# A graph layer on one Trainium2 core: five picked stretches and 25 gathered chunks per 125 chunks, in place of four and 45

## Chip, core and metric

The kernel runs on one core of a Trainium2 chip. The metric is the device time of one execution in microseconds (us), the median over repeated runs. Before the change it is 2684.04 us over 14 runs, which lie between 2659.6 and 2693.91 us.

A core has engines that run side by side, each through its own list of instructions in order: TensorE (PE; its weight loads are shown apart as PEld), VectorE (DVE), ScalarE (ACT), GpSimd (POOL) and SyncE (SP), which only issues DMAs here. An engine waits where an instruction needs what another has not finished yet. TensorE writes to PSUM, and DVE or ACT have to take its results from there.

## What is computed

A message layer over a graph of 12,500 nodes with 128 features and 400,000 edges, sorted by target node:

```python
Xs = X[src]
m_data = Xs @ W_data.T + b_data
m_ctrl = Xs @ W_control.T + b_control
msg = jnp.where((edge_types == 0)[:, None], m_data, m_ctrl)
agg = jax.ops.segment_sum(msg, dst, num_segments=X.shape[0])
out = jax.nn.relu(agg + (X @ W_self.T + b_self))
result = _layernorm(X + out)
```

Everything is float32. `src` and the edge types are random; `dst` is sorted, so a stretch of edges belongs to a narrow band of target nodes.

## The kernel before, in words

The sums are formed first and multiplied by the weights afterwards: for every target node and both edge types the kernel adds up the rows `x[src]` and counts the edges, and the 128x128 weight products are done once for each node.

**Chunks, groups, stretches.** A chunk is 128 edges (`P`), and there are 3125 of them (`NC`). A group is 125 chunks (`GC`), and there are 25 groups (`NG`). Inside a group the generator `windows(g)` (line 160) lets two kinds of stretches alternate: a *gathered* stretch of `PC[i]` chunks and a *picked* stretch of `EC` = 20 chunks. With `PC = (12, 11, 11, 11)` a group has four of each, 45 gathered chunks and 80 picked ones. `NE = len(PC)` is the number of pairs in a group, and there are `NG * NE` = 100 pairs in all.

**The rows.** `x` is split once into three bfloat16 parts (high, middle, low), which together keep its float32 value. They stay in SBUF as `x3` (99 blocks of 128 nodes) and are also written to DRAM as `rows3`, 768 bytes for each node.

**A gathered chunk** (`gathered`, line 648) fetches its 128 source rows from DRAM. POOL issues one indirect DMA for each chunk (line 660) into a tile `msg` that holds `SB` = 4 chunks; six such tiles rotate (`bufs=6`, line 855). DVE builds a 0/1 matrix `psel` of 128 edges by 2 x 24 nearby target nodes (line 653 through line 443). TensorE then adds the three parts with three matmuls of 48 columns (line 616) and the counts with a fourth (line 674), each with its own 128x128 weight load. All chunks of a stretch add into one PSUM tile `sums`, and DVE adds that to `acc` at the stretch's end (line 646).

**A picked stretch** (`picked`, line 680, and `give_slots`, line 451) brings its 2560 edges' rows together without a DMA of rows. The edges are sorted by the block of 128 nodes in which their source lies: each of 98 blocks gets 32 slots, and up to 64 edges that find their block full go to an overflow list. The ranks of the edges inside their blocks come from 20 matmuls (`before`, line 483) and a series of DVE steps (lines 491 to 537). A second series of 20 matmuls (`put`, line 550) writes node and code of each edge into its slot. The node numbers go to DRAM and come back as `pick`, repeated over all 128 partitions (`spread`, lines 560 and 562, 800 KB), and DVE turns them into a 0/1 matrix (line 601). TensorE picks the rows out of `x3` with 98 matmuls of 384 columns that use 32 columns of the array each (`got`, line 694), for 25 tiles of 128 slots. ACT copies two such tiles at a time from PSUM to SBUF (`emsg`, line 705). TensorE adds them up with 75 matmuls of 176 columns (line 616) and counts with 25 (line 721). The overflow rows are fetched by one indirect DMA of 64 rows (`last`, line 713).

**The order.** Everything is recorded by hand: for each picked stretch `w` the function `merged` (line 137) sorts small units of work by a given place between 0 and 1 and runs them in that order. Merged are the seven units ("turns") of `picked(w)`, the slots of stretches `w+2` and `w+3`, the 0/1 matrix of `w+1`, the loads and preparations for the next groups, the closing of the previous group, and the gathered chunks, which are spread evenly over the whole program with a lag of two stretches (`LAG`, line 870). Each engine runs its part of the list in this order. A gathered chunk's DMAs are recorded where its `msg` tile begins, and POOL runs ahead of the matmuls as far as free `msg` tiles, free `last` tiles (two) and finished overflow lists (`idx`, line 589) let it.

**Loads and closing.** `load(g, kind)` (line 176) fetches sources, targets and types of a group's stretches, one DMA for each gathered stretch and array, and is issued two groups ahead from SP. Line 174 checks that all stretches of a kind stand 31 chunks apart, and `load` uses that 31 as its stride. `finish` (line 762) multiplies a group's sums by the weights, 125 nodes at a time, normalizes and writes out; for the last group, `soon` (line 759) says which blocks of nodes are closed after the last pair but one and which after the last. If an overflow list or a band of nodes would not fit, flags (lines 909 to 923) send the program to a slow general path, `long_path`.

Of the kernel before, what the change touches and what calls it, by code (L numbers as in the profile page):

```python
# [17 lines left out]
P = 128  # L18
# [4 lines left out]
GC = 125  # L23
NG = NC // GC
GN = P * GC * N // E
PC = (12, 11, 11, 11)
PB = 12
EC = 20
CQ = 4
NE = len(PC)  # L30
NWIN = 2 * NE
LAG = 2
DPC = P * N // E
PAD = 10
PW = DPC + 2 * PAD
EW = 88
AW = PW + DPC * (PB - 1)
WMAX = max(AW, EW)
# [5 lines left out]
NCELL = 4 * NQ  # L44
OVF = 64
TOP = 7
SB = 4
ACC_ROWS = 99 * P
EPS = 1e-5

assert sum(PC) + NE * EC == GC and NC % GC == 0 and NBLK == NCELL - 2 and max(PC) == PB


@with_exitstack
def kernel(
# [50 lines left out]
    with ExitStack() as sx:  # L106
        short_path(sx, tc, const, ident, eps, wT, brow, bad, x, src, dst, etype,
                   (w_data, w_ctrl, w_self), (b_data, b_ctrl, b_self), out)
# [38 lines left out]
def short_path(ctx, tc, const, ident, eps, wT, brow, bad, x, src, dst, etype, ws, bs, out):  # L147
    nc = tc.nc
# [11 lines left out]
    def windows(g):  # L160

        c = g * GC
        for i, n in enumerate(PC):
            yield "p", i, c, n
            yield "e", i, c + n, EC
            c += n + EC

    def edges(a, c, n):
        return a[c * P:(c + n) * P].rearrange("(p c) -> p c", c=n)

    rows_p = NE * PB
    raw = {}
    starts = {k: [c for kind, _, c, _ in windows(0) if kind == k] for k in "pe"}
    assert all(b - a == 31 for k in "pe" for a, b in zip(starts[k][k == "p":], starts[k][1 + (k == "p"):]))

    def load(g, kind):
        names = ("src", "dst", "typ")
        if kind == "e":
            raw[kind, g] = [ld.tile([P, NE, EC], I32, name=f"e{name}") for name in names]
            c = g * GC + starts["e"][0]  # L180
            for t, a in zip(raw[kind, g], (src, dst, etype)):
                at = a[c * P:(c + 31 * (NE - 1)) * P].rearrange("(i k) -> i k", k=31 * P)[:, :EC * P]
                nc.sync.dma_start(out=t[:, :NE - 1, :], in_=at.rearrange("i (p c) -> p i c", c=EC))
                nc.sync.dma_start(out=t[:, NE - 1, :], in_=edges(a, c + 31 * (NE - 1), EC))
        else:
            raw[kind, g] = [ld.tile([rows_p, P], I32, name=f"p{name}") for name in names]
            c = g * GC
            for t, a in zip(raw[kind, g], (src, dst, etype)):
                nc.sync.dma_start(out=t[:PB, :], in_=a[c * P:(c + PB) * P].rearrange("(c p) -> c p", p=P))
                for i in range(1, NE):  # L190
                    b = c + starts["p"][i]
                    nc.sync.dma_start(
                        out=t[i * PB:(i + 1) * PB, :], in_=a[b * P:(b + PB) * P].rearrange("(c p) -> c p", p=P)
                    )
# [11 lines left out]

    load_first("e")
    load(0, "e")
    load_first("p")


    near_i = keep.tile([rows_p, NG], I32, name="near_i")
    for kind, i, c, _ in windows(0):
        if kind == "p":
            nc.sync.dma_start(
                out=near_i[i * PB:(i + 1) * PB, :],
                in_=dst.rearrange("(o g e) -> o g e", o=1, g=NG)[:, :, c * P].to_broadcast([PB, NG]),
            )
    load(0, "p")


# [392 lines left out]
    def add_rows(out, msg, sel, start, stop):  # L614
        for j in range(3):
            nc.tensor.matmul(  # L616
                out, msg[:, j * D:(j + 1) * D], sel, start=(start and j == 0), stop=stop, skip_group_check=True
            )
# [29 lines left out]
    def gathered(g, i):  # L648
        n = PC[i]
        s = {}  # L650

        def choose():
            sel = sp.tile([P, n, 2 * PW], BF, name="psel")
            s["sel"] = select(sel, near_col, codes["p", g][1][:, i * PB:i * PB + n])

        def chunk(c):
            if c % SB == 0:
                s["msg"] = mp.tile([P, SB, 3 * D], BF, name="msg")
                for k in range(min(SB, n - c)):
                    nc.gpsimd.indirect_dma_start(  # L660
                        out=s["msg"][:, k, :], out_offset=None, in_=rows3[:, :],
                        in_offset=bass.IndirectOffsetOnAxis(
                            ap=codes["p", g][0][:, i * PB + c + k:i * PB + c + k + 1], axis=0
                        ),
                    )
            if c == 0:
                s["ps"] = sums()
                choose()
            sel = s["sel"][:, c].rearrange("p (t w) -> p t w", t=2)
            rows, cnt = (  # L670
                cells_of(s["ps"], AW, k).rearrange("p (t w) -> p t w", t=2)[:, :, DPC * c:DPC * c + PW] for k in range(2)
            )
            add_rows(rows, s["msg"][:, c % SB, :], sel, c == 0, c == n - 1)
            nc.tensor.matmul(cnt, one_col, sel, start=False, stop=(c == n - 1), skip_group_check=True)  # L674
            if c == n - 1:
                accumulate(g, 2 * i, s["ps"], AW, PW + DPC * (n - 1))

        return evenly([lambda c=c: chunk(c) for c in range(n)])
# [77 lines left out]

    soon = {NE - 2: (0, 1), NE - 1: (2, 3, 4)}
    assert (starts["p"][NE - 1]) * DPC - PAD >= 2 * (P - 3)  # L760

    def finish(g, ks):
        full = P - 3
# [85 lines left out]
    prep_e(0)  # L849
    merged(evenly(all_slots(0) + all_slots(1)), evenly(split_units))  # L850
    load(1, "e")
    load(1, "p")
    early.close()
    pro.close()
    mp = ctx.enter_context(tc.tile_pool(name="msg", bufs=6))
    sp = ctx.enter_context(tc.tile_pool(name="sel", bufs=2))
    fp = ctx.enter_context(tc.tile_pool(name="fin", bufs=2))
    merged(pick_matrix(0))
# [8 lines left out]
    for p in range(pairs):  # L867
        g, i = divmod(p, NE)
        for c, (_, u) in enumerate(gathered(g, i)):
            at = LAG + (p + (c + 0.5) / PC[i]) * (pairs - LAG) / pairs  # L870
            chunks.setdefault(int(at), []).append((at % 1, u))
        closed.setdefault(int(at), []).append(p)

    for w in range(pairs):
        g, i = divmod(w, NE)
# [188 lines left out]
```

## Time and profile before

| quantity | value |
|---|---|
| median of 14 runs | 2684.04 us (2659.6 to 2693.91) |
| the profiled execution | 2674.92 us |
| its span, first to last instruction | 2673.2 us |
| mean granted TensorE clock in it | 0.88 of full speed |
| instructions | 73115 |
| DVE busy | 1504.4 us, 4288 instructions |
| ACT busy | 1207.1 us, 2296 instructions |
| POOL busy | 1306.0 us, 1242 instructions |
| DMA moved | 236.87 MB, 89 GB/s on average |

The profile is of one execution. A group of instructions is shown by its line in the kernel, its engine, what it writes and reads, its shape and its count, then busy time, the mean length of one, and the idle time of the engine just before them with whoever ended it. "Issue" as the one who ended a wait means that the engine waited for nothing that the profile shows. The end of a matmul is modelled, so the distance from one matmul's start to the next tells more of TensorE's pace than the busy time does. The granted clock is what TensorE was given of its full clock. Of the chain of work that ended last, 62% is PE, 10% "issue", 10% a queue that the profile does not tell, 10% ACT and 5% DVE.

### The profile page before, as it was taken

The numbers are of one execution on the slowest core, as the hardware profiler recorded it, in microseconds if no ns is written. First come the engines' busy times: TensorE is split into PE (matmuls) and PEld (weight loads), VectorE is DVE, ScalarE is ACT, GpSimd is POOL, SyncE is SP. The second block draws the span as 40 slices with busy tenths as digits, with TensorE's granted clock in tenths as the row PEclk, the third lists the DMA queues.
The fourth block names the chain that finished last, engine by engine and source line by source line (L and its number), as shares of the span: only waits on it lengthen the run. The fifth ranks groups of instructions, "written<-read, shape, count | busy, mean of one in ns | idle before, by whom it ended". The sixth has DMA issues, their size and how long they took to land.

```text
span 2673.2 us, 73115 instructions
## 1 busy us (share of the span) xinstructions
PE 2090.1 (78%) x30669; PEld 1549.0 (58%) x30669; DVE 1504.4 (56%) x4288; ACT 1207.1 (45%) x2296; POOL 1306.0 (49%) x1242
## 2 busy tenths in 40 slices
PE   1678788788788887788888788787787887887877
PEld 0456566565566555665666566565565665665655
DVE  6665565555566555555555555564655555455542
ACT  3444445444454443444444444443544444444434
POOL 0544555545455554455455455445555545355451
PEclk9888999888888888888888888888999889888988
DMA  7433233222223332232232222232332222222221
GB/s 196 148 81 95 77 96 98 75 88 74 88 84 91 93 86 82 78 92 79 90 90 85 92 81 85 83 90 80 88 93 79 90 84 85 82 75 93 74 84 43
DMA packets 184175, 236.87 MB, mean 89 GB/s; under 512 B 79440, under 2 KB 151436, under 8 KB 183836
## 3 DMA queue, kind: packets, MB, share of 16 engines
q0 software_dynamic: 57200, 115.59, 15.6%
q1 hardware_dynamic: 113554, 109.92, 12.9%
q10 hardware_dynamic: 13082, 6.60, 0.9%
q8 instruction: 242, 3.96, 0.6%
q14 instruction: 97, 0.79, 0.1%
HBM read 215.35 MB, written 16.64 MB: 87 GB/s over the span
## 4 chain that ended last, share of the span: by engine, by line
PE 62%; issue 10%; another core or an unknown queue 10%; ACT 10%; DVE 5%; DMA 1%; POOL 0%; SPq 0%; DVEq 0%; ACTq 0%; POOLq 0%
PE sums L616 26%; PE got L694 20%; ACT emsg L705 7%; PE fin L800 4%; PE rk L483 3%; PE rk L550 2%; PE sums L721 2%; PE rk L575 1%; PE sums L674 1%; DMA xt<-in_x_dram 1%; DVE esel L443 1%; ACT h L829 1%; PE rk L570 1%; DVE prod L495 1%
## 5 line engine op out<-in xcount | busy, mean ns | idle before, releaser
L660 POOL DMA_INDIRECT msg<-rows,pidx x1125 | 1208.4, 1074 | 1214.2 <-PE sums L616 655.2
L705 ACT CAST emsg<-got 128x768 bf16<-128x768 f32 x1200 | 913.8, 802 | 916.4 <-PE got L694 365.4
L616 PE MATMUL sums<-esel,emsg 128*128 128x176 bf16 x7200 | 788.7, 261 | 99.7 <-issue 96.5
L694 PE MATMUL got<-x,pick 128*32 128x384 bf16 x9800 | 679.0, 364 | 160.1 <-ACT emsg L705 84.9
L616 PEld LDWEIGHTS <-emsg 128*128 128x128 bf16 x7200 | 610.4, 107 | 247.5 <-issue 242.5
L443 DVE TENSOR_TENSOR esel<-code_col,code 128x1408 bf16<-128x1408 bf16 (+1 forms) x400 | 291.9, 730 | 326.1 <-PE sums L616 166.7
L694 PEld LDWEIGHTS <-pick 128*32 128x32 bf16 x9800 | 248.6, 99 | 344.4 <-issue 249.4
L616 PE MATMUL sums<-psel,msg 128*128 128x48 bf16 x3375 | 251.3, 191 | 52.5 <-issue 42.1
L616 PEld LDWEIGHTS <-msg 128*128 128x128 bf16 x3375 | 206.1, 102 | 92.5 <-issue 86.4
L443 DVE TENSOR_TENSOR O<-cell_col,blk 128x2000 bf16<-128x2000 bf16 x100 | 118.1, 1181 | 210.5 <-issue 210.2
L721 PE MATMUL sums<-esel,one_col 128*32 128x176 bf16 x2500 | 182.0, 259 | 38.6 <-issue 37.1
L674 PE MATMUL sums<-psel,one_col 128*128 128x48 bf16 x1125 | 190.1, 189 | 12.0 <-issue 11.9
L483 PE MATMUL rk<-O,ltri 128*128 128x100 bf16 x2000 | 144.8, 230 | 60.1 <-issue 31.1
L491 DVE TENSOR_REDUCE ahead<-rk 128x100 bf16<-128x400 f32 x100 | 57.4, 574 | 230.5 <-remote 76.2
L483 PEld LDWEIGHTS <-ltri 128*128 128x128 bf16 x2000 | 120.2, 109 | 94.4 <-issue 59.1
L550 PE MATMUL rk<-rv,O 128*128 128x64 bf16 x2000 | 104.0, 205 | 58.9 <-issue 57.1
L713 POOL DMA_INDIRECT last<-rows,idx x100 | 93.6, 936 | 108.4 <-DMA xs<-in_x_dram 78.2
L721 PEld LDWEIGHTS <-one_col 128*32 128x32 bf16 x2500 | 89.2, 105 | 96.9 <-issue 67.6
L550 PEld LDWEIGHTS <-O 128*128 128x128 bf16 x2000 | 80.8, 105 | 107.5 <-issue 97.8
L585 ACT CAST code<-rk 128x50 bf16<-128x50 f32 x200 | 35.3, 176 | 228.4 <-PE rk L575 115.0
L545 DVE TENSOR_SCALAR om<-slot_col,rk 128x448 bf16<-128x448 bf16 x100 | 35.5, 355 | 178.3 <-PE rk L541 82.6
L601 DVE TENSOR_SCALAR pick<-pick,lane_f 128x1600 bf16<-128x1600 bf16 x200 | 127.0, 636 | 7.9 <-DMA pick<-there 5.3
(156 smaller groups left out, 2129.8 us busy)
## 6 DMA issues: line engine op xcount, KB each, us to landing
pick<-there SPq DMA_DIRECT2D x100, 800.0 KB
msg<-rows,pidx POOLq DMA_INDIRECT x1125
rows<-x SPq DMA_DIRECT2D x6, 1344.0 KB
xs<-in_x_dram SPq DMA_DIRECT2D x99, 62.5 KB
out_dram<-h SPq DMA_DIRECT2D x99, 62.5 KB
xt<-in_x_dram ACTq DMA_DIRECT2D x6, 896.0 KB
psrc<-in_src_dram SPq DMA_DIRECT2D x100, 6.0 KB
pdst<-in_dst_dram SPq DMA_DIRECT2D x100, 6.0 KB
```

The lines of the kernel that those rows point to most:

```text
L443: nc.vector.tensor_tensor(sel.rearrange("p n (w t) -> p n w t", t=2), col[:rows].rearrange("p (o w t) -> p o w t", o=1, t=2).to_broadcast( ...
L483: nc.tensor.matmul(cols[:, :, cells], ltri[:, a, :], s["O"][:, j:j + CQ, cells], start=(a == 0 and j == 0), stop=(j == EC - CQ), skip_grou ...
L550: nc.tensor.matmul(s["rk"][:, :2 * CAP], s["held"][:, c * NCELL:c * NCELL + P], s["rv"][:, c].rearrange("p v r -> p (v r)"), start=(c == 0 ...
L601: nc.vector.tensor_scalar(t, t, lane_f, None, op0=OP.is_equal)
L616: nc.tensor.matmul(out, msg[:, j * D:(j + 1) * D], sel, start=(start and j == 0), stop=stop, skip_group_check=True)
L660: nc.gpsimd.indirect_dma_start(out=s["msg"][:, k, :], out_offset=None, in_=rows3[:, :], in_offset=bass.IndirectOffsetOnAxis(ap=codes["p", ...
L674: nc.tensor.matmul(cnt, one_col, sel, start=False, stop=(c == n - 1), skip_group_check=True)
L694: nc.tensor.matmul(ps[CAP * a:CAP * (a + 1), :], slots[w]["pick"][:, a * NQ + q, :], x3[:, 4 * q + a - a0].rearrange("p j d -> p (j d)"), ...
L705: nc.scalar.copy(msg, ps[:, :, :3 * D])
L713: nc.gpsimd.indirect_dma_start(out=msg[:OVF, :], out_offset=None, in_=rows3[:, :], in_offset=bass.IndirectOffsetOnAxis(ap=slots[w]["idx"], ...
L721: nc.tensor.matmul(cells_of(s["ps"], EW, 1)[CAP * (q % 4):CAP * (q % 4 + 1), :], one_col[:, :CAP], s["sel"][q], start=(q < 4), stop=(q + 4 ...
L800: nc.tensor.matmul(s["ph"][:rows, i * D:(i + 1) * D], left, right, start=(j == 0), stop=(j == len(terms) - 1))
```

## The change

A group of 125 chunks is divided into five pairs in place of four: `PC` becomes `(5, 5, 5, 5, 5)`, with 20 picked chunks behind each. So there are 125 picked stretches in place of 100, and 625 gathered chunks in place of 1125. A `msg` tile holds five chunks, a whole gathered stretch, and four of them rotate in place of six of four chunks. The stride of stretches of one kind is 25 chunks in place of 31, and is now computed. For the last group three blocks of nodes are closed after the last pair but one and two after the last, in place of two and three. All widths that follow from these numbers (tables by `NE`, `PB`, `NWIN`, the width `AW` of a gathered stretch's sums) change with them. From line 172 on the changed kernel's lines have numbers higher by one.

```diff
-PC = (12, 11, 11, 11)
-PB = 12
+PC = (5, 5, 5, 5, 5)
+PB = 5
...
-SB = 4
+SB = 5
...
-    assert all(b - a == 31 for k in "pe" for a, b in zip(starts[k][k == "p":], starts[k][1 + (k == "p"):]))
+    gap = GC // NE
+    assert all(b - a == gap for k in "pe" for a, b in zip(starts[k][k == "p":], starts[k][1 + (k == "p"):]))
...
-                at = a[c * P:(c + 31 * (NE - 1)) * P].rearrange("(i k) -> i k", k=31 * P)[:, :EC * P]
+                at = a[c * P:(c + gap * (NE - 1)) * P].rearrange("(i k) -> i k", k=gap * P)[:, :EC * P]
                 nc.sync.dma_start(out=t[:, :NE - 1, :], in_=at.rearrange("i (p c) -> p i c", c=EC))
-                nc.sync.dma_start(out=t[:, NE - 1, :], in_=edges(a, c + 31 * (NE - 1), EC))
+                nc.sync.dma_start(out=t[:, NE - 1, :], in_=edges(a, c + gap * (NE - 1), EC))
...
-    soon = {NE - 2: (0, 1), NE - 1: (2, 3, 4)}
-    assert (starts["p"][NE - 1]) * DPC - PAD >= 2 * (P - 3)
+    soon = {NE - 2: (0, 1, 2), NE - 1: (3, 4)}
+    assert (starts["p"][NE - 1]) * DPC - PAD >= 3 * (P - 3)
...
-    mp = ctx.enter_context(tc.tile_pool(name="msg", bufs=6))
+    mp = ctx.enter_context(tc.tile_pool(name="msg", bufs=4))
```

## The prediction

> **What bounds the kernel now.** First the page: which engine is busiest, and with what.
>
> ```profile
> span 2673.2 us, 73115 instructions
> PE 2090.1 (78%) x30669; PEld 1549.0 (58%) x30669; DVE 1504.4 (56%) x4288; ACT 1207.1 (45%) x2296; POOL 1306.0 (49%) x1242
> ...
> L660 POOL DMA_INDIRECT msg<-rows,pidx x1125 | 1208.4, 1074 | 1214.2 <-PE sums L616 655.2
> L705 ACT CAST emsg<-got 128x768 bf16<-128x768 f32 x1200 | 913.8, 802 | 916.4 <-PE got L694 365.4
> ```
>
> POOL and ACT mostly wait for PE, so PE sets the pace. Next the view of who PE waits for:
>
> ```profile
> PE sums L616 <- issue: 141.0, 292, 1.2
> PE got L694 <- ACT emsg L705: 84.9, 191, 1.5
> PE got L694 <- issue: 59.8, 130, 1.2
> PE rk L550 <- issue: 57.1, 100, 1.4
> ```
>
> All PE waits that name another engine come to 161 us after the first pick; those for nothing shown ("issue") to 347 us. Whether the second kind belongs to picked or to gathered work decides this case. Stretches of time (length, then busy PE, PEld, DVE, ACT, POOL with counts, granted clock, DMA share, GB/s):
>
> ```profile
> 84.00:104.00 20.00, 18.43 (x317) 13.35 (x315) 19.93 (x59) 14.03 (x25) 17.26 (x10) 1.00 0.34 105
> 106.00:124.00 18.00, 7.45 (x45) 3.56 (x44) 2.02 (x6) 1.60 (x2) 13.74 (x15) 0.64 0.28 76
> 2630.00:2656.00 26.00, 24.20 (x417) 18.72 (x414) 6.64 (x17) 17.40 (x27) 0.00 (x0) 1.00 0.02 5
> 1097.40:1100.80 3.40, 2.99 (x30) 1.98 (x30) 3.37 (x7) 2.86 (x5) 2.63 (x3) 0.50 0.28 77
> ```
>
> From 106 us POOL issues 15 gathers back to back (1.25 us apart), and PE gets 45 matmuls done in 18 us. After 2630 us POOL is silent: 417 matmuls in 26 us, full clock, and no "issue" wait at all. At 84 to 104 us the gathers come 2 us apart, and PE runs freely. POOL's timeline shows the usual pattern, runs of gathers:
>
> ```profile
> 1009.42 0.95 POOL L660 DMA_INDIRECT msg<-rows,pidx  x1 [7.10 <-PE sums L616]
> 1010.67 0.95 POOL L660 DMA_INDIRECT msg<-rows,pidx  x1 [0.30 <-issue]
> 1011.93 0.95 POOL L660 DMA_INDIRECT msg<-rows,pidx  x1 [0.30 <-issue]
> 1013.18 0.95 POOL L660 DMA_INDIRECT msg<-rows,pidx  x1 [0.31 <-issue]
> ```
>
> I laid the "issue" idles over 0.1 us (768, together 355 us) on POOL's runs (gaps under 1 us). Runs, moved 2 us later, cover 1609 us of the span and hold 354.8 of the 355.1 us. So PE starves while gathers are in flight, a few us into a run; its clock then falls. The loss belongs to runs of gathers. What undisturbed work costs, from PE's timeline at full clock:
>
> ```profile
> 86.59 0.83 PE L694 MATMUL got<-x,pick 128*32 128x384 bf16 x16
> 87.25 0.25 PE L721 MATMUL sums<-esel,one_col 128*32 128x176 bf16 x4
> 87.44 1.08 PE L616 MATMUL sums<-esel,emsg 128*128 128x176 bf16 x12
> 88.45 0.83 PE L694 MATMUL got<-x,pick 128*32 128x384 bf16 x16
> ...
> 1047.26 0.23 PE L616 MATMUL sums<-psel,msg 128*128 128x48 bf16 x3
> 1047.34 0.18 PE L674 MATMUL sums<-psel,one_col 128*128 128x48 bf16 x1
> 1047.45 0.83 PE L694 MATMUL got<-x,pick 128*32 128x384 bf16 x16
> ```
>
> Start to start: 16 picks 0.66 us, 4 counts 0.19, 12 sums 1.01, a gathered chunk 0.19.
>
> **The ledger before.** A picked stretch, undisturbed: 98 picks 4.04, 25 counts 1.19, 75 sums 6.31, the 20 matmuls of line 483 1.04 (94.69 to 95.73 us), the 20 of line 550 0.58 (92.43 to 93.01), lines 570 and 575 0.45 (93.48 to 93.93): 13.6 us. A gathered chunk: 0.10 to 0.20 in such places; I take 0.15. Closing 100 blocks of nodes: 1.4 us each, from the three at the end (2658.1 to 2663.0 us, a small one among them); 140 us. So 100 x 13.6 + 1125 x 0.15 + 140 = 1669 us of work. PE has 2673.2 less 71 before the first pick and 7 after its last instruction: 2595. Lost: 926 us, 161 of it to other engines, and 765 to the runs: starving, and the low clock behind it.
>
> What a run costs: between 1 us after its first gather and 3 us after its last (or the next run), I added each matmul's distance to the next less what that pair takes undisturbed. 41 runs of three: 1.4 us on average; 127 of four 2.9; 56 of five 4.2; 18 of eight (two of four with a small gap) 5.2; 10 of nine 7.0. About 0.5 of each is waits for other engines, counted above: 0.9, 2.4, 3.7, 4.7, 6.5. With the first run of 26 (24 us) that makes some 750 us, which agrees.
>
> **The change, part by part.**
>
> *25 more picked stretches* add 25 x 13.6 = 340 us of PE work. Waits for other engines go with them: 161 x 1.25 = 201. DVE gets (1504 - 78 before 100 us) / 100 = 14.3 us a stretch, so some 1850 us; ACT (1207 - 47) / 100 = 11.6, so some 1500. Both stay below PE's 1.25 x 13.6 x 100 = 1700 plus the rest; ACT is the nearer one in a free stretch (17.40 of 26 us above). If it held PE up more often, half as much again on 161 would be 80 us, and no row shows less than the share of now; 0 and 40 are my ends for the extra, and I take 0. The 25 more `pick` broadcasts (800 KB) are hidden: they are issued a stretch before they are needed, and PE's waits for `pick` are two, both before 75 us.
>
> *500 fewer gathered chunks* take 500 x 0.15 = 75 us off (50 to 100 by the bounds). DVE's `psel` (430 ns, 100 of them) and stretch sums (416 ns for 256 columns) become 125 smaller ones, off PE's path.
>
> *Preparations by group*: `load` issues 15 small DMAs for gathered stretches where it issued 12, the tables at the start 2 and 1 more; all on SP, two groups ahead or beside the loading of `x` before 71 us. 0 us; each could cost at the start at most the length of one small landing, some 2 us (`there`'s landing is waited for 62.3 us in 57 waits, 1.1 each): 0 to 6 us.
>
> *The end*: two blocks in place of three behind the last stretch, 1 us less.
>
> *The runs.* POOL's list in the changed program repeats `last`, then five `msg`, for every stretch. `last` of stretch w waits for its overflow list, made at the end of stretch w-2, and for its buffer, read at the same point. Behind it five gathers are queued whose tile (four rotate) was read out a stretch or more earlier: nothing holds them. So each stretch gets one run of six at its start; before, the six smaller tiles came free one by one and gave runs of three to five, 2.6 a stretch. The gathers now released are ready two stretches early, so nobody waits for them. Gathers fall from 1225 to 750, but runs grow. A run of six is not in the trace. Lower end: the starving goes by the gather and the low clock by the run. The excess ended by "issue" in that tally is 509 us, 0.42 for each gather, and the rest of 765 is 256, 1.0 for each of 256 runs; 6 x 0.42 + 1.0 = 3.5, and since `last` brings 64 rows and not 128, 3.4. Upper end: the step from four to five (1.3) goes on: 5.0. From five to nine the step is 0.7, so 4.4, which I take: it is nearest to the rows beyond five. 125 x 4.4 = 550 us.
>
> Sum: 71 + 7 + 1700 + 625 x 0.15 + 140 + 201 + 550 - 1 = 2762 us, against 2673 by the same ledger. The median lies 2684.04 / 2674.92 = 1.0034 above the profiled execution, so 2771; I say 2770.
>
> Two pages of the Trainium skill bear on the runs. The page "Runtime: NRT & Kernel Launch" (Instruction fetch mechanics) says that instructions come in blocks of 16 KiB and that this is mostly hidden; the trace has 242 packets of that queue (3.96 MB) and yet 347 us in which PE waits for nothing shown, so the rule as it stands does not hold here. By it the runs' starving, if it is one of instructions, would be hidden, and the ledgers without runs (2212 and 1908 us) would make the change 304 us slower. The page "TensorE: Matmul & The Clock Gate" (The HAM clock gate) says that the clock is either full or half, and halves after an idle window of about 3.4 us; the slice from 1097.4 us has 0.50 for 3.4 us. By that rule a run of six, if it starves PE so long, halves the clock once in every stretch, an estimate of 125 x 1.7 = 213 us from the page's figures.
>
> **The rivals.**
>
> *Faster: the starving goes by the gathered row.* Then a run costs 3.4 us and the sum is 2762 - 125 x 1.0 = 2637, 2646 as a median. For it: runs of eight cost 0.6 a gather, no more than the average of now (765 / 1225 = 0.62), and fewer runs are fewer falls of the clock. Against: 0.9, 2.4, 3.7 for three, four, five is far from proportional. Place: the start of each picked stretch. It decides below (2673 - 2212) / 125 = 3.7 us a run, 2212 being the sum without runs.
>
> *Much slower: runs of six starve PE to the end.* At 5.0 us a run, and ACT holding PE up half as often again (40 us of the 80), 2762 + 75 + 40 = 2877, 2887 as a median. For it: 45 matmuls in 18 us in the long run. Against: that run has 15 full gathers on end.
>
> *Slower by the average stretch.* If the loss went with picked work, a gathered chunk at its mean distance (0.29, waits included) leaves (2595 - 140 - 326) / 100 = 21.3 us a stretch: 25 x 21.3 - 500 x 0.29 = 388 more, 3071 as a median. Against: the free stretch after 2630 us.
>
> *It does something else*: a flag sends it to the slow path. From the inputs the fullest overflow list has 63 of 64 places (57 before), the fullest lane 5 of 7, the widest band 84 of 88; so not.
>
> **How the numbers follow.** Forecast (3.7 to 4.8 us a run) 0.52, faster rival 0.28, much slower 0.14, average stretch 0.05, the rest 0.01. What this measurement can tell from no change is about 0.3%, 8 us. The faster rival reaches into that with 0.06 of its 0.28, the forecast with 0.02: faster 0.22, same 0.08, slower 0.70. The range runs from the lower end of the runs' cost, 2645, to 2865, which is short of the full upper case; about 0.08 is left out below and 0.12 above. The forecast's own range is 2685 to 2820 (3.7 to 4.8).
>
> **What would show it.** POOL: 625 `msg` and 125 `last`, in runs of six that begin where `last` is released. PE: "issue" idles in one place of each stretch, 350 to 450 us in all, and a stretch of some 21 us from first pick to first pick. ACT: 1500 casts, the wait of picks for them near 106 us. Wrong if the issue idle falls below 300 us (faster rival) or the picks wait over 150 us for ACT; wrong in its root if "issue" idles appear outside the runs.

## The result, with the profile after

The changed kernel takes 2823.52 us, the median of 10 runs (2811.1 to 2844.36); the kernel before took 2682.33 us over 47 runs beside it. The ratio is 1.0542, with an interval of 1.0513 to 1.0571: slower by 141 us. The profiled execution took 2827.83 us at a span of 2826.1 us. The forecast was 2770 us.

Chips differ in this case. On three of the chips of the experiments the kernel before takes 1915 us, on another 2690 us, much as in the result; every ratio below is to the kernel before on the same chip.

The page of the changed kernel: first the engines, then the groups that answer to those shown of before (busy time, mean ns of one, idle time before them and what ended most of it).

```profile
span 2826.1 us, 82925 instructions
...
PE 2293.2 (81%) x34919; PEld 1718.6 (61%) x34919; DVE 1793.6 (63%) x5167; ACT 1459.1 (52%) x2746; POOL 798.5 (28%) x767
...
L706 ACT CAST emsg<-got 128x768 bf16<-128x768 f32 x1500 | 1142.9, 802 | 911.1 <-PE got L695 412.6
L661 POOL DMA_INDIRECT msg<-rows,pidx x625 | 672.8, 1077 | 1810.5 <-PE sums L675 1243.3
...
L714 POOL DMA_INDIRECT last<-rows,idx x125 | 121.6, 973 | 173.9 <-DMA ptyp<-in_edge_type_dram 77.8
```

PE is busier, with a quarter more casts on ACT and 500 gathers fewer on POOL, as the diff says. The means of one cast (802 ns) and one gather (1077 ns, 1074 before) have hardly changed. What PE waits for (us in total, times, longest):

```profile
PE got L695 <- ACT emsg L706: 128.1, 135, 6.3
PE got L695 <- issue: 81.3, 105, 9.8
PE sums L617 <- issue: 77.7, 149, 1.2
PE rk L551 <- issue: 52.3, 93, 1.2
```

The waits that end with "issue" fell from 347 us to 270 us in all, but picks now wait 128 us for ACT, against 85 us. POOL's timeline (start, length, then in brackets the idle time before and who ended it) shows a whole run:

```profile
1011.42 1.01 POOL L661 DMA_INDIRECT msg<-rows,pidx  x1 [14.95 <-PE sums L675]
1012.74 0.98 POOL L661 DMA_INDIRECT msg<-rows,pidx  x1 [0.30 <-issue]
1014.02 0.94 POOL L661 DMA_INDIRECT msg<-rows,pidx  x1 [0.30 <-issue]
1015.27 0.95 POOL L661 DMA_INDIRECT msg<-rows,pidx  x1 [0.30 <-issue]
1016.53 0.98 POOL L661 DMA_INDIRECT msg<-rows,pidx  x1 [0.30 <-issue]
1017.81 0.97 POOL L714 DMA_INDIRECT last<-rows,idx  x1 [0.30 <-DVE top L513]
1036.20 1.70 POOL L661 DMA_INDIRECT msg<-rows,pidx  x1 [17.42 <-ACT emsg L706]
```

One run of six, then nothing for 17 us, then the next run. Stretches of time around that run (length, then busy PE, PEld, DVE, ACT, POOL with counts, granted clock, DMA share, GB/s):

```profile
1014.00:1017.00 3.00, 1.88 (x29) 1.10 (x27) 1.92 (x7) 0.00 (x0) 2.37 (x3) 1.00 0.26 73
1017.00:1020.00 3.00, 0.73 (x4) 0.47 (x5) 2.77 (x14) 0.00 (x0) 1.48 (x2) 1.00 0.29 77
1020.00:1023.40 3.40, 3.34 (x22) 3.32 (x22) 1.88 (x11) 2.13 (x5) 0.00 (x0) 0.62 0.29 30
...
1027.00:1030.00 3.00, 2.94 (x58) 2.25 (x56) 2.76 (x14) 2.08 (x5) 0.00 (x0) 1.00 0.00 0
```

This is the loss in four rows. From the third gather on PE gets 29 matmuls done in 3 us, then 4; ACT does nothing at all, while DVE works on. Then the work comes back, but the clock has fallen: 0.62 is the mean of a row in which PE had half speed from 1020.84 us on, for 3.4 us. Seven microseconds later all is well again (58 matmuls in 3 us). PE's own timeline in the second and third row:

```profile
1017.22 0.24 PE L722 MATMUL sums<-esel,one_col 128*32 128x176 bf16 x1 [1.06 <-issue]
...
1018.63 0.31 PE L617 MATMUL sums<-esel,emsg 128*128 128x176 bf16 x2 [1.00 <-issue]
1020.06 0.84 PE L617 MATMUL sums<-esel,emsg 128*128 128x176 bf16 x9 [1.11 <-issue]
```

Twelve matmuls that belong together, and take 1.01 us undisturbed, are broken up by pauses of a microsecond in which nothing that the profile shows is missing.

What ACT waits for at that place is called "remote", which means that its wait ended with a signal whose sender the view could not name:

```profile
1012.30 1.54 ACT L706 CAST emsg<-got 128x768 bf16<-128x768 f32 x2
1020.31 1.50 ACT L706 CAST emsg<-got 128x768 bf16<-128x768 f32 x2 [6.46 <-remote]
```

The trace's semaphore records tell the sender: the cast at 1020.31 us follows a signal of PE at 1020.24, and the last pick before it that raises this signal ended, as modelled, at 1016.10.

Where the time came from and went, by the same count as in the prediction (each matmul's distance to the next, less what such a pair takes undisturbed; the excess is put down to what ended the pause, and the excess without a pause to the low clock). The first row is the ledger's prices times the counts (125 x 13.6 + 625 x 0.15 + 140 for the changed kernel), so it is reckoned and not measured, and the small rows below it are rough:

| us of PE's steady time | before | after | difference |
|---|---|---|---|
| undisturbed work | 1669 | 1934 | +265 |
| excess ended by "issue" | 509 | 369 | -140 |
| low clock | 257 | 223 | -34 |
| excess ended by ACT's casts | 121 | 159 | +38 |
| the rest | 39 | 60 | +21 |
| sum | 2595 | 2745 | +150 |

The remaining 3 us of the spans' difference (152.9) lie before the first pick, after the last matmul and in rounding. So by this table the change pays 265 us of work and gets back only 115 us of the loss to gathers. Two of its rows can be checked another way. In the stretches at half speed, matmul distances without a pause exceed what such pairs take on a chip without the loss by 281 us before and 245 after, which is near the table's -34. PE's pauses over 0.1 us that name another engine than ACT's casts are 75 us before and 63 after, so the +21 of the last row is not confirmed.

### The profile page after: what moved, and what is told of

Its sections match the earlier page's. It is cut to its first block, busy times and chain, and to the rows that moved or that the text cites. A ratio compares the mean times of both kernels' runs of the same rounds, so it can differ in the third digit from the quotient of the medians.

```text
span 2826.1 us, 82925 instructions
## 1 busy us (share of the span) xinstructions
PE 2293.2 (81%) x34919; PEld 1718.6 (61%) x34919; DVE 1793.6 (63%) x5167; ACT 1459.1 (52%) x2746; POOL 798.5 (28%) x767
## 4 chain that ended last, share of the span: by engine, by line
PE 61%; DVE 11%; another core or an unknown queue 10%; ACT 8%; issue 7%; DMA 2%; SPq 0%; DVEq 0%; ACTq 0%
PE sums L617 26%; PE got L695 18%; ACT emsg L706 6%; PE fin L801 4%; PE rk L484 4%; PE rk L551 3%; PE sums L722 2%; DVE esel L444 1%; DVE pick L602 1%; PE rk L576 1%; DVE prod L496 1%; DMA pick<-there 1%; DMA xt<-in_x_dram 1%; DVE rm L444 1%
## 5 line engine op out<-in xcount | busy, mean ns | idle before, releaser
L706 ACT CAST emsg<-got 128x768 bf16<-128x768 f32 x1500 | 1142.9, 802 | 911.1 <-PE got L695 412.6
L661 POOL DMA_INDIRECT msg<-rows,pidx x625 | 672.8, 1077 | 1810.5 <-PE sums L675 1243.3
L617 PE MATMUL sums<-esel,emsg 128*128 128x176 bf16 x9000 | 936.2, 258 | 65.9 <-issue 63.7
L695 PE MATMUL got<-x,pick 128*32 128x384 bf16 x12250 | 785.9, 353 | 222.4 <-ACT emsg L706 128.1
L617 PEld LDWEIGHTS <-emsg 128*128 128x128 bf16 x9000 | 747.2, 105 | 252.5 <-issue 248.7
L444 DVE TENSOR_TENSOR esel<-code_col,code 128x1408 bf16<-128x1408 bf16 (+1 forms) x500 | 364.9, 730 | 408.2 <-PE sums L617 240.8
L695 PEld LDWEIGHTS <-pick 128*32 128x32 bf16 x12250 | 294.0, 98 | 432.9 <-issue 303.4
L617 PE MATMUL sums<-psel,msg 128*128 128x48 bf16 x1875 | 159.0, 189 | 16.9 <-issue 14.0
L496 DVE TENSOR_TENSOR prod<-O,ahead 128x2000 bf16<-128x2000 bf16 x125 | 149.5, 1196 | 2.6
L617 PEld LDWEIGHTS <-msg 128*128 128x128 bf16 x1875 | 126.3, 102 | 29.9 <-issue 26.8
```

Of the source, the lines that this page charges most:

```text
L444: nc.vector.tensor_tensor(sel.rearrange("p n (w t) -> p n w t", t=2), col[:rows].rearrange("p (o w t) -> p o w t", o=1, t=2).to_broadcast( ...
L496: nc.vector.tensor_tensor(prod, s["O"], ahead.rearrange("p (o j) -> p o j", o=1).to_broadcast([P, EC, NCELL]), op=OP.mult)
L617: nc.tensor.matmul(out, msg[:, j * D:(j + 1) * D], sel, start=(start and j == 0), stop=stop, skip_group_check=True)
L661: nc.gpsimd.indirect_dma_start(out=s["msg"][:, k, :], out_offset=None, in_=rows3[:, :], in_offset=bass.IndirectOffsetOnAxis(ap=codes["p", ...
L695: nc.tensor.matmul(ps[CAP * a:CAP * (a + 1), :], slots[w]["pick"][:, a * NQ + q, :], x3[:, 4 * q + a - a0].rearrange("p j d -> p (j d)"), ...
L706: nc.scalar.copy(msg, ps[:, :, :3 * D])
```

## The experiments

### What is left where the gathers disturb nobody

The first question was what the runs are worth. One pair of kernels leaves the gathers of `msg` out; another has tiles of one chunk, so that gathers are released singly. The edits, for the kernels without gathers and for those with small tiles (before: `SB = 4` to 1, `bufs=6` to 24):

```diff
-                s["msg"] = mp.tile([P, SB, 3 * D], BF, name="msg")
-                for k in range(min(SB, n - c)):
-                    nc.gpsimd.indirect_dma_start(
...
+                s["msg"] = still
...
-    mp = ctx.enter_context(tc.tile_pool(name="msg", bufs=4))
+    still = keep.tile([P, SB, 3 * D], BF, name="still")
+    nc.vector.memset(still, 0.0)
```

```diff
-SB = 5
+SB = 1
...
-    mp = ctx.enter_context(tc.tile_pool(name="msg", bufs=4))
+    mp = ctx.enter_context(tc.tile_pool(name="msg", bufs=20))
```

> The changed kernel without the 625 gathers of msg: its matmuls read one tile of zeros, so the gathered edges' rows are left out of the sums; the 125 gathers of last stay. If the loss belongs to runs of gathers (forecast), TensorE's waits for nothing shown fall from 273 us to under 30, and the time falls by the excess that lies in the runs, some 600 us, to 2210-2270 us. If the loss belongs to picked work (the rival by the average stretch), the time stays within 50 us of 2823.

> The kernel before without the 1125 gathers of msg, which leaves the gathered edges' rows out of the sums in the same way. Forecast: 2682 less some 740 us, 1920-1990 us, and the changed kernel without gathers stands some 300 us above it (340 for 25 picked stretches, 75 less for gathered chunks, 40 for waits). If the loss belongs to picked work: 2630-2680.

> The changed kernel with msg tiles of one chunk, 20 of them in place of four of five: the same gathers, rows and buffer space, but each gather is released by a matmul of its own. If the length of a run decides (forecast), the runs of six break up into ones and twos, which cost next to nothing, and the time falls to 2230-2400 us. If the loss goes by the gathered row (the faster rival's premise, 0.6 us a gather), it stays within 60 us of 2823.

> The kernel before with msg tiles of one chunk, 24 of them in place of six of four. If the length of a run decides, the runs of three to five break up; 1225 gathers at 1.25 us are 1530 us, so they stand closer than in the changed kernel and some starving may stay: 2000-2350 us. If the loss goes by the gathered row: within 60 us of 2682.

They came on a chip where the kernel before takes 1915.4 us, so that the ratios answer another question than the one asked:

| kernel | us | ratio to before | interval |
|---|---|---|---|
| after without gathers | 2158.02 | 1.1272 | 1.1213 to 1.1331 |
| before without gathers | 1848.73 | 0.9656 | 0.96 to 0.9713 |
| after, one-chunk tiles | 2200.22 | 1.1503 | 1.1453 to 1.1553 |
| before, one-chunk tiles | 1923.14 | 1.0041 | 1.0013 to 1.0069 |

On this chip PE has, in all four kernels together, one pause over 0.1 us that ends with "issue" (0.2 us), and the granted clock is 0.98 or more on the mean of each profiled execution, even where up to 287 gathers follow each other with no gap of a microsecond (in before with one-chunk tiles). Leaving the gathers out saves 67 us in the kernel before. So the next experiment ran the changed kernel itself, and its small tiles again, on such a chip.

> The changed kernel itself beside the kernel before on one chip. The four runs so far fell on a chip on which the kernel before takes 1915 us and no wait of TensorE for nothing shown lies in its gather runs. If this run falls on such a chip, the ledger without runs holds: before 1915, this one 1915 plus 340 for 25 picked stretches less 75 for 500 gathered chunks, some 2180, ratio 1.13 to 1.15. If it falls on a chip like the first, 2823 against 2682, ratio 1.05. If picked stretches were not the price (loss by gathers alone), the ratio on the free chip would be near 1.00.

> The changed kernel with 20 msg tiles of one chunk, again. On a chip that starves TensorE during gather runs: 2230-2400 us if the length of a run decides, within 60 us of 2823 if the loss goes by the gathered row. On a free chip: within 1% of the changed kernel, since no run costs anything there.

The changed kernel took 2191.21 us against 1914.97, a ratio of 1.1458 (1.1397 to 1.1518): 276 us slower, where the table of work above gives 265. With one-chunk tiles it took 2195.86 us (1.1492, 1.1426 to 1.1557), which is the same. Lines of the changed kernel's page, its waits of PE and POOL's timeline on this chip:

```profile
span 2182.0 us, 82925 instructions
...
PE 1970.1 (90%) x34919; PEld 1556.2 (71%) x34919; DVE 1776.0 (81%) x5167; ACT 1453.8 (67%) x2746; POOL 876.3 (40%) x767
...
PEclk9999999999999999999999999999999999999999
```

```profile
PE rk L542 <- DVE over_n L517: 128.7, 96, 21.8
...
PE got L695 <- ACT emsg L706: 7.9, 28, 0.4
```

```profile
1000.56 0.96 POOL L661 DMA_INDIRECT msg<-rows,pidx  x1 [7.46 <-PE sums L675]
1001.82 0.95 POOL L661 DMA_INDIRECT msg<-rows,pidx  x1 [0.30 <-issue]
1003.08 0.95 POOL L661 DMA_INDIRECT msg<-rows,pidx  x1 [0.30 <-issue]
1004.33 1.34 POOL L661 DMA_INDIRECT msg<-rows,pidx  x1 [0.30 <-issue]
```

The same runs of six (115 of them, 119 in the result), 1.25 us from gather to gather in the lines shown, and none of PE's unexplained pauses. Two things follow. First, a run of gathers does not by itself stop PE: it is a property of some chips that PE starves in it. Second, with the same 1500 casts the picks wait 7.9 us for ACT and not 128.1. The 128 us are no lack of ACT's speed; they come with the runs. The trace of the result shows how: in its idle times, ACT's casts wait 371 us (115 times) for a "remote" signal, which never occurs in this run. Laid on POOL's runs moved 2 us later, which cover 985 us of the span, ACT's idles after 75 us that end with "remote" or "issue" fall inside them for 405 of 418 us.

The missing signal is PE's. After 75 us the trace of the result keeps 3020 signals of PE, and 360 of them come more than 1 us after the modelled end of the last matmul that raises them, 358 of these in or up to 4 us behind a run. In this run it is 2 of 3018. ACT's and DVE's signals are that late twice each in both traces, at the end of the program. So ACT does not stop by itself in the runs: it waits for PE, whose work is reported late, and PE in turn waits for ACT. Since the ends of matmuls are modelled, the trace does not say whether the matmul ended late or only its signal.

What holds PE up most in the undisturbed kernel can be read there too: DVE is at 81%, and PE's largest wait is for the ranks' sums (`over_n`).

The next experiment asked whether the tile sizes have a part of their own: the changed kernel with the old tiles (`SB = 4`, `bufs=6`), and the kernel before with five-chunk tiles (`SB = 5`, `bufs=5`).

> The changed kernel with the old msg tiles, six of four chunks: of the change only the split into five pairs of 20 picked and 5 gathered chunks is left. A stretch's gathers then come as four and one. On a free chip (before near 1915): within 1% of the changed kernel, 2170-2215 us, since tiles cost nothing there. On a chip that starves TensorE in gather runs (before near 2680): runs of four or five in place of six, 100-250 us under the changed kernel's 2823 if the length of a run decides, within 60 us of it if the loss goes by the gathered row.

> The kernel before with msg tiles of five chunks, five of them: of the change only the tiles. On a free chip: within 1% of the kernel before. On a starving chip: runs of five (a stretch of 12 as 5, 5, 2, one of 11 as 5, 5, 1) in place of four, 50-150 us over 2682 if the length of a run decides, within 30 us if the loss goes by the gathered row.

On a chip where before takes 1915.33 us they took 2184.74 us (1.1452, 1.1331 to 1.1573) and 1919.22 us (1.0033, 1.0007 to 1.006). Undisturbed, the split into five pairs makes the whole difference, and the tiles make next to none. The runs did not come as expected: with the old tiles 117 of 126 are runs of six, so here they follow from the split and not from the tiles' size. Where gathers disturb, neither of the two kernels was run, so the tiles' own part there is not known from them.

### The two kinds of work apart, where the gathers disturb

Then a chip on which before takes 2689.73 us. Both kernels without their whole gathered side, so that only picked stretches, preparations and closing are left:

```diff
-        def choose():
...
         def chunk(c):
-            if c % SB == 0:
...
+            pass
...
-    mp = ctx.enter_context(tc.tile_pool(name="msg", bufs=4))
```

> The kernel before without its whole gathered side: no gathers, no 0/1 matrices, no matmuls and no sums of gathered chunks, whose edges are left out of the result. Measures the gathered chunk on TensorE. Without the gathers alone it took 1849 us; if a gathered chunk costs 0.15 us of TensorE (the ledger), 1125 of them come off: 1680 us. If they lie in gaps that other waits leave anyway, 1760-1849.

> The changed kernel without its whole gathered side, in the same way. Without the gathers alone it took 2158 us. Ledger: 625 x 0.15 off, 2064 us; the difference to the kernel before without its gathered side is 25 picked stretches, 340 us by their undisturbed work alone, some 385 with their waits for DVE and ACT.

They took 1713.59 us (0.6364, 0.6322 to 0.6405) and 2082.55 us (0.7734, 0.7684 to 0.7784), 34 and 19 us over what the ledger gave. Page and waits of PE of the first:

```profile
span 1711.2 us, 62013 instructions
...
PE 1544.4 (90%) x26169; PEld 1187.5 (69%) x26169; DVE 1404.6 (82%) x4088; ACT 1198.5 (70%) x2296; POOL 97.3 (6%) x117
```

```profile
PE rk L541 <- DVE over_n L516: 86.4, 65, 21.8
...
PE got L671 <- ACT emsg L682: 8.4, 28, 0.6
```

No pause of PE over 0.1 us ends with "issue", the mean clock is 0.994, and the picks wait 8.4 us for ACT, on the chip on which they starve when gathers run. The 25 stretches more cost 2082.55 - 1713.59 = 369 us, 14.8 us each, 1.2 over the 13.6 of work in the ledger. The gathered side is the rest of each whole kernel: 2689.7 - 1713.6 = 976 us before, 2823.5 - 2082.6 = 741 us after. Its own work is small: the kernels without gathers, which keep the gathered matmuls, lie 135 us (1848.7 - 1713.6, for 1125 chunks) and 75 us (2158.0 - 2082.6, for 625) above those without the gathered side, 0.12 us a chunk. So gathers that disturb cost 841 us before and 666 us after, and the change comes out as +369 for picked work, -60 for gathered work and -175 for the disturbance: +134 us, where 141 were measured. The last two terms set kernels from different chips against each other (without gathers on a chip at 1915 us, without the gathered side on the one at 2690), and no kernel without gathers ran on both kinds, so they are estimates.

### The same gathers, released singly

One question of the prediction was left: does the loss go by the gathered row or by the run? The one-chunk tiles again, now on the chip with before at 2689.26 us. Number, size and order of the gathers stay; only what they wait for is finer.

> The kernel before with 24 msg tiles of one chunk, again, for a chip that starves TensorE in gather runs. There (before near 2690) leaving the whole gathered side out gave 1714, so 976 us lie in the gathers and their chunks. If the length of a run decides: gathers are released one by one, and the time falls by 200 us or more, to 2000-2490. If the loss goes by the gathered row: 2630-2750. On a free chip (before near 1915): within 1% of it, as before.

> The changed kernel with 20 msg tiles of one chunk. On a starving chip: 2230-2500 us if the length of a run decides, since most gathers then come in ones and twos (on a free chip 114 twos and 124 ones), 2760-2880 if the loss goes by the gathered row. On a free chip: within 1% of 2191.

| kernel | us | ratio to before | interval |
|---|---|---|---|
| before, one-chunk tiles | 2318.48 | 0.8625 | 0.8571 to 0.8679 |
| after, one-chunk tiles | 2324.36 | 0.8635 | 0.8587 to 0.8682 |

POOL's timeline of the changed kernel with one-chunk tiles, then its waits of PE:

```profile
1013.21 0.95 POOL L661 DMA_INDIRECT msg<-rows,pidx  x1 [0.30 <-issue]
1016.61 1.98 POOL L661 DMA_INDIRECT msg<-rows,pidx  x1 [2.45 <-PE sums L617]
1023.08 1.41 POOL L661 DMA_INDIRECT msg<-rows,pidx  x1 [4.50 <-PE sums L617]
1026.91 1.58 POOL L661 DMA_INDIRECT msg<-rows,pidx  x1 [2.43 <-PE sums L617]
```

```profile
PE rk L542 <- DVE over_n L517: 92.5, 70, 21.9
PE rk L551 <- issue: 22.6, 35, 1.2
PE got L695 <- ACT emsg L706: 22.5, 48, 3.5
```

The same 625 gathers of `msg` with pauses between them: "issue" pauses over 0.1 us fall from 272.9 to 62.4 us, the picks' wait for ACT from 128 to 22.5 us, the mean clock rises from 0.885 to 0.966, and the kernel takes some 500 us less than the 2823.52 of the result. By length of run, the "issue" excess is 0.01 us for one gather alone, 0.06 for two, 0.06 for three, 0.18 for four, and 3.98 for the four runs of six that are left. In the kernel before the release is less even; its timeline and waits:

```profile
1003.64 0.94 POOL L660 DMA_INDIRECT msg<-rows,pidx  x1 [1.29 <-PE got L694]
1005.37 1.04 POOL L660 DMA_INDIRECT msg<-rows,pidx  x1 [0.79 <-PE sums L616]
1006.72 1.38 POOL L660 DMA_INDIRECT msg<-rows,pidx  x1 [0.30 <-issue]
```

```profile
PE got L694 <- ACT emsg L705: 78.3, 151, 9.6
PE sums L616 <- issue: 70.0, 179, 1.1
PE got L694 <- issue: 60.9, 147, 4.5
```

There 426 of 1225 gathers have a pause of 0.7 us or more ahead of them, against 277 with the larger tiles, and the median distance from gather to gather is 1.72 us in place of 1.30; some 280 us of "issue" excess are left of 509. (In the kernel after, 458 of 750 have such a pause against 125, and the distance is 2.04 us in place of 1.26.) So on this chip the loss goes by how closely gathers follow each other, not by how many there are, nor by the picked work. Both kernels come out alike: with one-chunk tiles the change's 25 stretches more and its 500 gathers less cancel on this chip. The better of the versions is the kernel before with one-chunk tiles: it takes 14% off here, and costs 0.4% (0.1 to 0.7%) where nothing starves, while the changed kernel with them costs 15% there.

## Why the prediction was near, and where it was off

**Undisturbed work.** 13.6 us for a picked stretch and 0.15 for a gathered chunk gave +265 us. The table of the result uses these prices and so is no test of them, but the experiments are: 276 us between the two kernels on one chip without starving, 14.8 us a stretch with waits (13.6 + 1.6 by the ledger), 0.12 us a chunk. The work was priced rightly. The ledgers without runs, 1908 and 2212 us, were a computed state; the chips without starving show it, at 1915 and 2191 us. That these are so near is in part luck: the ledgers held 161 and 201 us of waits for other engines, most of them for ACT's casts. Where nothing starves, PE's waits are 150 us in the kernel before (with five-chunk tiles) and 147 us in the changed one, most of them for the ranks' sums on DVE.

**The loss belongs to runs of gathers.** Right, and now shown by taking the gathers and their matmuls away (0.64 of the time), and by spacing the gathers (0.86). In the changed kernel 272.9 of 272.9 us of "issue" pauses fall into the runs moved 2 us later, so the sign "wrong in its root" did not come.

**A run of six costs 4.4 us.** This is the term that was sized too small. All that PE lost after the first pick is 2745 - 1934 = 811 us. PE's waits that name another engine, counted as in the prediction, are 191 us of it. That leaves 620 us for the runs, or 5.0 for each of the 125 stretches, where the sum had 550; it is the upper end that the prediction gave. The table, which goes by distances, gives 369 + 223 = 592 us, or 4.7. So carrying on with the step from five to nine came out too low. The 119 runs of six in the trace after show a part of why: their excess is 5.08 us on average, and 1.4 of it are waits for other engines (1.2 for ACT's casts), where the prediction took 0.5 off each run. And a spell at half clock is 6.8 us long in the median, against 3.4 before: of 654 us at half clock only 338 lie in the stretches that this count looks at, where it was 450 of 643 before. The first run, which was not counted apart, has 22 gathers and costs 27 us.

**Waits for other engines, 161 x 1.25 = 201 us, extra taken at 0.** The size was 10 us too large (191), but the reason was wrong. These waits were scaled with picked stretches, as if ACT's casts came late for being many: those for the casts rose from 86 to 128 us, the others fell from 75 to 63. Where nothing starves, 1500 casts make PE wait 7.9 us. Of the 128 us, 116 stand behind casts that had themselves waited for a signal of PE that came over 0.2 us late or that the view calls "remote". So these are PE's own late signals coming back to it through ACT, and should have been priced with the runs. 70 us too little for the runs, 10 too much for the waits and 4 us of smaller terms are the 64 us between the sum of 2762 and the span of 2826.1.

**From the profiled execution to the median.** The factor 1.0034 of before went the other way this time: 2823.52 / 2827.83 = 0.9985, which took 14 us off the miss. So 2823.52 us lies inside the range of 2645 to 2865, and 4 us beyond the 2685 to 2820 that the forecast had for itself.

**What releases a run.** The prediction had `last` as the gate, with five gathers behind it. The timeline shows the reverse: the `msg` tile is the gate, freed by the count matmul of an earlier gathered stretch (PE sums L675, 97 of the runs, 1243 us), and `last` comes sixth, 0.30 us behind the fifth. The run is still one of six, so the sum took no harm; but that step points to `last`'s buffers for a remedy, where nothing was tried, and the remedy that was shown to work sits at the `msg` tiles.

**The signs.** "Issue" pauses were to be 350 to 450 us and came to 270, below the 300 that was named as the sign of the faster rival. The time did not follow, since the sign counted one of three parts: the low clock and the waits for ACT's casts kept their share. Per run of six it is 2.1 us of pauses, 2.9 of "issue" excess, 5.1 of all excess. The stretch was to be 21 us and is 22.0 on average.

**The rivals.** *Faster* needed less than 3.7 us a run; it is 4.7 to 5.0, and the loss by the gathered row falls with the last experiment, where equal gathers cost 500 us less. *Much slower* had 5.0 a run and 40 us more for ACT: by the prediction's own count its first half came true, but the waits in all did not rise above 201 us. The forecast's 4.4 was thus no better than this rival's 5.0, and lower waits and the last factor kept the sum near it. *By the average stretch* (+388 us) falls with the picked kernels: picked work pays 14.8 us a stretch, not 21.3. *Something else* did not happen.

The page "Runtime: NRT & Kernel Launch" (Instruction fetch mechanics) of the Trainium skill says that going on from one block of instructions to the next is mostly hidden. On the chips at 1915 us nothing contradicts this: PE has next to no pause without a shown cause. On the chip at 2690 us it stops for a microsecond and more with nothing shown missing, and starts again. Whether it is its instructions that come late was not tried, so the prediction's words that the rule does not hold here are not shown.

**Open.** Why gathers that follow each other closely starve PE on some chips and not on others. The distance of gathers in a run is nearly the same on both (medians 1.26 us in the result, 1.27 without starving). No experiment separated instructions that come late from matmuls that are themselves held up and end later than modelled, or POOL's making of descriptors from the packets' way through the DMA engines. One sign favours the second: in the result and in its kernel before, 65 matmuls with a signal on record stand just ahead of an unexplained pause over 0.3 us, and 62 of the signals came late too, by over 0.05 us.

## What to carry to other kernels

Where an engine pauses and the profile names no cause, lay the pauses on the other engines' timelines: here all lay in runs of POOL's gathers, and only a part of the loss showed as pauses, the rest as a low clock and as waits for another engine that itself waited for PE's late signals. Price such a loss by the run, all three parts together, and look first for what lets transfers go off in a bunch: a tile of one transfer's size releases them singly, which took 14% and 18% off two kernels where gathers disturb, with no work moved. Weigh a change on more than one chip: this one costs 5% where gathers disturb, and 15% where they don't.

## What was not expected of the hardware

The same program takes 1915 us on some chips and 2690 on another, and each figure repeats: medians of 1914.97 to 1915.4 us on three chips, 2689.73 and 2689.26 us in two sets of runs on the other.

The clock follows the starving: 0.88 on average with it, 0.98 to 0.99 without, for the same instructions. In the windows shown, it fell to half after 6 us in which PE was busy for 2.6 us with 33 matmuls, with no pause longer than 1.11 us. The page "TensorE: Matmul & The Clock Gate" (The HAM clock gate) names an idle window of about 3.4 us as what halves the clock; these rows show a fall with no pause of that length. The prediction's estimate from it, 213 us, is close to the 223 us of the table by chance: it reckons with 125 falls of 3.4 us, and the trace has 102 spells at half clock, 654 us in all.

Closely spaced gathers hold up PE, and the other engines where they wait for it: DVE was busy for 2.77 of the 3 us in which PE did 4 matmuls and ACT, without PE's signal, nothing.
